# A hashed attention and feed-forward kernel on one core: the opening's weight loads, scales, filler products and first maxima rearranged

## The chip, the core and the metric

The kernel runs on one core of a Trainium2 chip. The core has five engines that run their own instruction streams in order: TensorE (PE) multiplies matrices, VectorE (DVE) and ScalarE (ACT) work elementwise, GpSimd (POOL) works elementwise too, and SyncE (SP) issues transfers. ScalarE can issue transfers as well (ACTq in the profile). The metric is the device time of one execution in microseconds; lower is better.

## What is computed

The input x has 16 batches of 512 tokens with 128 features. Each batch goes through an attention with 16 heads of 8 features and then through a feed-forward network (FFN) with a hidden width of 512:

```python
x = x + layernorm(attn(layernorm(x)))
x = x + layernorm(ffn(layernorm(x)))

def attn(x):                       # per batch and head
    q = x @ Wq.T + bq;  v = x @ Wv.T + bv
    bucket = sum over n of (q . hyperplane_n + offset_n >= 0) * 2**n
    coeff  = 62 + (bucket_i == bucket_j)
    a = softmax(q @ q.T / sqrt(128) * coeff)
    return a @ v

def ffn(x):                        # tlin(x, w, s) = (x @ w.T) * s, w ternary, s per output
    h = silu(tlin(x, w1, s1)) * tlin(x, w2, s2)
    h = gelu(tlin(h, h1, sh1));  h = gelu(tlin(h, h2, sh2))
    return tlin(h, w3, s3)
```

All is in float32, except that q is split into three bfloat16 parts for the scores.

## The kernel before

**Order.** The kernel isn't a loop nest. Processes written as generators (`prep`, `gathers`, `scores`, `coeffs`, `logits`, `maxima`, `softmax`, `attend`, `residual`, `ffn`, `weights`, `inputs`) are run by a small planner, class `Order` (L47 to L184), when the program is built. Each step names its engine, a cost in microseconds and a rank; at every moment the planner takes, on each engine that is free, the ready step of lowest rank (on ScalarE: of lowest ready time plus rank, with 4.0 added for a change of activation table), and emits its instructions. So the order of instructions on each engine, SP's transfers included, is fixed by the planner's costs. On the chip each engine follows that order and waits where its data are not there. Transfers cost the planner SP's issue time, a queue at 160 KB per microsecond and 2.6 us of latency.

**One batch.** `prep(b)` (L575) normalizes x, turns it over on TensorE, projects it to q (`qp`, L603), writes q with its bias as `qs` (L625) and as three bfloat16 parts (L708, L718, L723), each of which goes to DRAM in two layouts by two transfers (`keep`, L617). `buckets` (L628) makes the bucket numbers (`pp` L635, `bits` L647, `bkt` L662) and writes them to DRAM (`bkd`, L678). `prep` ends with v (`vp` L741, `vaug` L749). Batch 0 has its first transfer issued ahead of the planner.

**One head.** `gather(j)` (L768) fetches three tiles by SP: `ql` (L779), `qr` (L792) and the bucket row broadcast to all partitions, `bb` (L805). Four heads' tiles are there at once. For each of four groups of 128 rows, TensorE makes scores (`sp`, L827), VectorE the coefficients (`co`, L845) and the product of both with its row maxima (`l`, L874). The logits have 11 buffers of 128x2048. After two heads (`MH = 2`, L862 and L893) `maxima` (L899) turns the maxima over (`mt`, L903), writes them to DRAM (`md`, L908), and each head's `softmax` (L913) fetches them broadcast to all partitions (`mb`, L920). GpSimd subtracts them (`l`, L927), ScalarE takes the exponential (L932). After four heads `attend` (L937) multiplies by v on TensorE (`av`, L953), copies the result (`avs`, L967), turns it over (`op`, L974) and divides (L984, L985).

**After 16 heads** `residual(b)` (L998) normalizes the attention's output and adds x, in that order: mean and variance on VectorE (L423, L427), `ve` on ScalarE (L439), a power on GpSimd (`rs_o`, `rs_f`, L443), the rescaling on ScalarE (L466). Then `ffn(b)` (L1021) runs: the gates `w1` and `w2` (L1066), silu (L1052), their product (L1036), two layers `hp` (L1100) with gelu (L1113), and `yp` (L1132). Its steps on TensorE have the rank 4, behind scores (0), `av` (1) and `prep` (2). `ffn(0)` waits for the event `loaded`.

**Weights.** `weights` (L1166) loads five weights by SP, each with its scales broadcast to all partitions (L1185, L1186: 256 KB of scales for each of w1, w2, h1 and h2, 64 KB for w3), and GpSimd multiplies the scales into the weights (L1189). The first three are started at once, the last two wait for the event `gathered[3]` (`EARLY`, `LATER`). `inputs` (L503) takes the statistics of the later batches' x on ScalarE (L523, L533).

Of the kernel before, what the change touches and what calls it, by code (L numbers as in the profile page):

```python
# [46 lines left out]
class Order:  # L47
# [62 lines left out]
    def _step(self, p, value):  # L110
        while True:
            self.current = p
            try:
                want = p.gen.send(value)
            except StopIteration:
                self.live -= 1
                return
            value = None
            if want[0] == "get":
                pool = want[1]  # L120
                if not pool.free:
                    pool.waiters.append(p)
                    return
                value, deps = pool.free.pop(0)
                self._merge(p, deps)
            elif want[0] == "wait":
                if want[1].deps is None:
                    want[1].waiters.append(p)
                    return
                self._merge(p, want[1].deps)  # L130
            else:
                eng = want[1]
                when = max(
                    [self.now] + [
                        t + (self.LAT if e != eng else 0.0 if e in ("PE", "SP") else self.OWN)
                        for e, t in p.deps.items()
                    ]
                )
                self._at(when, self._offer, p, want, when)
                return  # L140
# [47 lines left out]
def tile_lsh_attention_ffn(  # L188
# [35 lines left out]
    ROOT = float(np.float32(E**-0.5))  # L224
    GROUPS = (1, 2, 6, B)
    LATE = 20
    EARLY, LATER = 2, 3
    SCALE = 1.0 / math.sqrt(E)
    AHEAD = 1
    MH = 2  # L230
# [41 lines left out]
    nc.gpsimd.memset(eps3, EPS / E**3)  # L272

    junk = const.tile([P, E], BF16, name="junk")
    warm = const.tile([P, 1], F32, name="warm")
    nc.scalar.activation(warm, eps, AF.Exp)

# [56 lines left out]
    def act(cost, rank, emit, table=None):  # L334
        return ("op", "ACT", cost, emit, rank, table)
# [239 lines left out]
    def prep(b):  # L575
# [46 lines left out]
            yield dma(256, 1, emit, cost=0.7)  # L622
            od.set(kept[i])

        yield act(0.65, -2, lambda: nc.scalar.activation(qs, qp, AF.Identity, bias=bq_sb))  # L625
        read = Event()

        def buckets():  # L628
            yield wait(read)
# [73 lines left out]

        wrote, columned = Event(), Event()
        od.spawn(buckets())
        od.set(read)
        yield act(
            0.65, -2, lambda: nc.scalar.activation(qparts[0], qp, AF.Identity, bias=bq_sb)  # L708
        )
        od.spawn(keep(0))  # L710
        yield dve(
            0.63,
            1,
# [54 lines left out]
    def gather(j, tag):  # L768
        b, h = divmod(j, H)
        yield wait(prepared[b])  # L770
        ql = p1.tile([KS, S], BF16, tag=f"ql{tag}", name=f"ql_{j}")
        qr = p1.tile([KS, S], BF16, tag=f"qr{tag}", name=f"qr_{j}")
        bb = p1.tile([P, BR * BP], BF16, tag=f"bb{tag}", name=f"bb_{j}")
        rows[j] = (ql, qr, bb, tag)

        yield dma(
            74,
            1 + j * 1e-3,
            lambda: nc.sync.dma_start(  # L779
                out=ql,  # L780
                in_=qds[b][1][h]
                .rearrange("i d s -> (i d) s")
                .unsqueeze(1)
                .to_broadcast([NP * DH, NP, S]),
            ),
            held=False,
            cost=0.75,
        )
        yield dma(
            74,  # L790
            1 + j * 1e-3,
            lambda: nc.sync.dma_start(  # L792
                out=qr,
                in_=qds[b][0][h]
                .rearrange("d j s -> (d j) s")
                .unsqueeze(0)
                .to_broadcast([NP, NP * DH, S]),
            ),
            held=False,
            cost=0.72,  # L800
        )
# [57 lines left out]
    def logits():  # L859
        for j in range(B * H):  # L860
            kl = yield get(logit_bufs)
            if j % MH == 0:  # L862
                km, pair = (yield get(mx_bufs)), []
                mx = mxpads[int(km[2:])]
            l = p1.tile([P, NT, S], F32, tag=kl, name=f"l_{j}")
            base = j % MH * NT
            for t in range(NT):
                i = j * NT + t
                yield wait(scored[i])
                yield wait(weighed[i])  # L870
# [13 lines left out]

                yield dve(0.61, 5, emit)
                od.put(score_banks, ks)
                od.put(co_bufs, kc)
                if t < NT - 1:
                    od.loose()
            od.put(row_bufs, rows.pop(j)[3])  # L890
            ls[j] = (l, kl)
            pair.append((j, l))
            if len(pair) == MH:  # L893
                od.spawn(maxima(pair, mx, km))
            if j % GH == GH - 1:
                od.spawn(attend(j // GH))
            od.loose()
# [123 lines left out]
    def ffn(b, x1, k1, xnt, kx):  # L1021
        if b:
            yield wait(stages[b - 1][AHEAD])
        yield wait(loaded)
        kh = yield get(h_bufs)
        h = p1.tile([P, NC, S], F32, tag=kh, name=f"h_{b}_0")
        there = events(NC)
# [14 lines left out]
        def silus(c0, gates, half, held):  # L1042
            for _ in gates:
                held.append((yield get(a_bufs)))
            tiles = [
                p1.tile([P, S], F32, tag=ka, name=f"a_{b}_{c0 + i}")
                for i, ka in enumerate(held)
            ]

            def emit():  # L1050
                for a, (_, gp) in zip(tiles, gates):
                    nc.scalar.activation(a, gp, AF.Silu)  # L1052

            yield act(1.2, 0, emit, "silu")
            for kb, _ in gates:
                od.put(ffn_banks, kb)
            held[:] = zip(tiles, list(held))
            od.set(half)
# [25 lines left out]
        for layer in (1, 2):  # L1084
# [5 lines left out]
            for c0 in range(0, NC, 2):  # L1090
# [16 lines left out]
                        )  # L1107
                    got.append((c, kb, hp))

                def gelus(got=got, h=h, there=there):  # L1110
# [54 lines left out]

    def weights():  # L1166

        kl = yield get(logit_bufs)
        scales = p1.tile([P, NT, S], F32, tag=kl, name="scales")
        scale3 = const.tile([P, E], F32, name="scale3")  # L1170
        folded = []
        for i, (src, scale, nk, n, name) in enumerate((
            (w1_t, w1_s, 1, HID, "w1"),
            (w2_t, w2_s, 1, HID, "w2"),
            (h1_t, h1_s, NC, HID, "h1"),
            (h2_t, h2_s, NC, HID, "h2"),
            (w3_t, w3_s, NC, E, "w3"),
        )):
            w_sb[name] = w = const.tile([P, nk, n], F32, name=name)
            sc = scales[:, i, 0:n] if i < NT else scale3  # L1180
            folded.append(Event())

            def fetch(w=w, sc=sc, src=src, scale=scale, nk=nk):
                for i in range(nk):
                    nc.sync.dma_start(out=w[:, i, :], in_=src[i * P : (i + 1) * P, :])  # L1185
                nc.sync.dma_start(out=sc, in_=scale.partition_broadcast(P))  # L1186

            def fold(w=w, sc=sc, nk=nk, n=n):
                nc.gpsimd.tensor_tensor(  # L1189
                    w, w, sc.unsqueeze(1).to_broadcast([P, nk, n]), op=ALU.mult  # L1190
                )

            def piece(fetch=fetch, fold=fold, nk=nk, n=n, done=folded[-1], i=i):
                if i > EARLY:
                    yield wait(gathered[LATER])
                yield dma(nk * n / 2 + n / 2, 3, fetch, cost=0.42 * (nk + 1))
                yield pool(nk * n / 450, 2, fold)
                od.set(done)

            od.spawn(piece())  # L1200
        for e in folded:
            yield wait(e)
        od.put(logit_bufs, kl)
        od.set(loaded)

    with tc.manual_schedule():
        for piece in (prep(0), gathers(), scores(), coeffs(), logits(), weights(), inputs()):
            od.spawn(piece)
        od.run()

# [51 lines left out]
```

## Time and profile before

| | us |
|---|---|
| median of 3 runs | 1388.59 |
| their range | 1387.49 to 1397.21 |
| the profiled execution, its own time | 1398.15 |
| its span, first to last instruction | 1396.3 |
| busy: TensorE, VectorE, GpSimd, ScalarE | 1287.3, 1235.2, 1227.3, 1110.4 |

The page gives busy time and its share of the span. Its part with 40 slices shows how this share changes in time, in tenths, and a row `PEclk` with the TensorE clock that was granted in each slice. Other views are asked for by a window in microseconds from the span's start: busy time by stretch, instructions in order of time (an entry in square brackets says how long the engine was idle before the instruction, and what ended that), and who waited for whom. Rows of SPq and ACTq are issues of transfers; their duration is that of the issue, not of the transfer.

### The profile page before, as it was taken

How to read it: one execution, taken by the hardware profiler on the slowest of the kernel's cores; microseconds unless marked ns; L12 is line 12 of the kernel's file. 1: busy time of each engine (PE TensorE's matmuls, PEld its weight loads, DVE VectorE, ACT ScalarE, POOL GpSimd, SP SyncE). 2: the span in 40 equal slices, each digit the busy share in tenths (PEclk: the TensorE clock that was granted, in tenths of full speed). 3: DMA queues.
4: the chain of work that ended last, by engine and by line, in shares of the span. 5: the costliest groups of instructions: out<-in, count | busy, mean ns of one | idle time of the engine just before them, and what ended most of it. 6: DMA issues, size and time to landing. Idle time of an engine off the chain costs nothing.

```text
span 1396.3 us, 20309 instructions
## 1 busy us (share of the span) xinstructions
PE 1287.3 (92%) x5520; PEld 521.9 (37%) x5520; DVE 1235.2 (88%) x3985; ACT 1110.4 (80%) x1608; POOL 1227.3 (88%) x322
## 2 busy tenths in 40 slices
PE   4677699899899999999999999999999999999997
PEld 1111133434344343433444334434343344433353
DVE  5978899899899999999999999999999999999220
ACT  3566789889879888988989888888888897878752
POOL 2699799989999998999999999998999899999700
PEclk9666699899999999999999999999999999999999
DMA  5655355455445445444445544454544544444100
GB/s 172 188 132 157 103 149 149 120 144 140 122 112 151 119 131 144 123 142 120 148 122 133 148 122 140 128 136 127 142 126 132 136 135 134 127 112 116 46 8 8
DMA packets 158418, 176.09 MB, mean 126 GB/s; under 512 B 32480, under 2 KB 115680, under 8 KB 158304
## 3 DMA queue, kind: packets, MB, share of 16 engines
q1 hardware_dynamic: 157872, 174.59, 45.6%
q8 instruction: 44, 0.72, 0.2%
q14 instruction: 70, 0.57, 0.2%
q10 hardware_dynamic: 432, 0.20, 0.0%
HBM read 155.59 MB, written 19.14 MB: 125 GB/s over the span
## 4 chain that ended last, share of the span: by engine, by line
PE 63%; DVE 21%; issue 6%; DMA 4%; POOL 3%; ACT 2%; SPq 0%; POOLq 0%; DVEq 0%
PE hp L1100 24%; PE av L953 16%; PE sp L827 12%; DVE l L874 10%; DVE co L845 7%; PE w L1066 3%; PE yp L1132 3%; POOL l L927 2%; DMA mb<-md 2%; PE op L974 1%; PE pp L635 1%; PE qp L603 1%; DMA ql<-qd 1%; PE vp L741 1%; ACT l L932 1%
## 5 line engine op out<-in xcount | busy, mean ns | idle before, releaser
L927 POOL TENSOR_TENSOR l<-l,mb 128x2048 f32<-128x2048 f32 x256 | 1156.3, 4552 | 36.4 <-DMA mb<-md 32.0
L874 DVE CUSTOM_DVE_ANT_0 l<-co,sp 128x512 f32<-128x512 bf16 x1024 | 666.2, 686 | 29.2 <-PE av L953 22.3
L932 ACT ACTIVATE l<-l 128x2048 f32<-128x2048 f32 x256 | 486.5, 1907 | 41.2 <-POOL l L927 40.0
L1100 PE MATMUL hp<-h,h 128*128 128x512 f32 x1024 | 495.5, 596 | 0.2 <-ACT h L1113 0.2
L845 DVE TENSOR_SCALAR co<-bb,bj 128x516 bf16<-128x516 bf16 x1024 | 454.9, 477 | 3.9 <-DMA bb<-bkd 3.8
L827 PE MATMUL sp<-qr,ql 72*128 72x512 bf16 x1024 | 378.3, 404 | 80.6 <-DVE mxpad L874 68.3
L953 PE MATMUL av<-l,vaug 128*32 128x512 f32 x2048 | 280.7, 636 | 0.4 <-DVE y L1156 0.2
L1100 PEld LDWEIGHTS hp<-h,h 128*128 128x128 f32 x1024 | 190.5, 190 | 176.0 <-issue 152.9
L827 PEld LDWEIGHTS <-ql 72*128 72x128 bf16 x1024 | 96.7, 99 | 410.6 <-issue 383.4
L1066 PE MATMUL w<-xnt_f,w 128*128 128x512 f32 x256 | 133.0, 616 | 3.2 <-ACT y L390 2.0
L932 ACT ACT_TABLE_LOAD x86 | 110.3, 1283 | 1.5
L967 ACT COPY avs<-av 128x512 f32<-128x512 f32 x64 | 37.3, 582 | 90.1 <-PE av L953 90.1
L1113 ACT ACTIVATE h<-hp 128x512 f32<-128x512 f32 x128 | 71.0, 595 | 33.9 <-PE hp L1100 33.3
L953 PEld LDWEIGHTS av<-l,vaug 128*32 128x32 f32 x2048 | 47.8, 112 | 123.0 <-issue 89.9
L874 DVE DVE_READ_ACCUMULATOR2_ANT mxpad<- 128x1 f32 x1024 | 91.6, 89 | 0.0
L1113 ACT ACT_TABLE_LOAD x58 | 74.4, 1283 | 0.8
L1132 PEld LDWEIGHTS yp<-w,h 128*128 128x128 f32 x512 | 67.0, 196 | 12.7 <-issue 8.1
L1036 DVE TENSOR_TENSOR h<-w,a 128x512 f32<-128x512 f32 x64 | 43.9, 687 | 27.8 <-PE w L1066 22.0
L1132 PE MATMUL yp<-w,h 128*128 128x128 f32 x512 | 67.9, 280 | 0.0
L1066 PEld LDWEIGHTS w<-xnt_f,w 128*128 128x128 f32 x256 | 47.6, 196 | 50.9 <-issue 21.5
L443 POOL TENSOR_TENSOR rs_y<-ve_y,mhalf 128x4 f32<-128x4 f32 x16 | 16.2, 1010 | 51.8 <-issue 34.7
L448 DVE TENSOR_SCALAR nm_y<-su_y,rs_y 128x1 f32<-128x1 f32 x64 | 9.2, 210 | 38.5 <-POOL rs_y L443 38.5
(91 smaller groups left out, 868.8 us busy)
## 6 DMA issues: line engine op xcount, KB each, us to landing
mb<-md SPq DMA_DIRECT2D x256, 256.0 KB
bb<-bkd SPq DMA_DIRECT2D x256, 130.5 KB
ql<-qd SPq DMA_DIRECT2D x256, 72.0 KB
qr<-qd SPq DMA_DIRECT2D x256, 72.0 KB
qd<-q SPq DMA_DIRECT2D x96, 128.0 KB
xta<-in_L_attn_x_dram SPq DMA_DIRECT2D x16, 256.0 KB
xtr<-in_L_attn_x_dram SPq DMA_DIRECT2D x16, 256.0 KB
out_dram<-y SPq DMA_DIRECT2D x16, 256.0 KB
```

The source lines that it names most:

```text
L827: nc.tensor.matmul(sp, lhsT=ql[:, ts(t, P)], rhs=qr, start=True, stop=True)
L845: nc.vector.tensor_scalar(co, bb.rearrange("p (r c) -> p r c", c=BP)[:, :, 0:BC], bjs[b][:, c : c + 1], float(NBKT - 2), op0=ALU.is_equal, ...
L874: nc.vector.tensor_tensor_reduce(out=l, in0=co[:, 0:S], in1=sp, scale=1.0, scalar=-3.0e38, op0=ALU.mult, op1=ALU.max, accum_out=mx[:, t : ...
L927: lambda: nc.gpsimd.tensor_tensor(l, l, mb.unsqueeze(1).to_broadcast([P, NT, S]), op=ALU.subtract),
L932: yield act(1.82, 0, lambda: nc.scalar.activation(l, l, AF.Exp, scale=SCALE), "exp")
L953: nc.tensor.matmul(av[k * Q : (k + 1) * Q, :], lhsT=va[:, t, c : c + Q], rhs=ls[gg * GH + k][0][:, t, :], start=(t == 0), stop=(t == NT - 1),)
L967: yield act(0.5, -2, lambda: nc.scalar.copy(avs, av))
L1036: lambda: nc.vector.tensor_tensor(h[:, c, :], g2, a, op=ALU.mult),
L1066: lambda: nc.tensor.matmul(gp, lhsT=w_sb[which][:, 0, ts(c, P)], rhs=xnt, start=True, stop=True),
L1100: lambda i=i: nc.tensor.matmul(hp, lhsT=w[:, i, ts(c, P)], rhs=hin[:, i, :], start=(i == 0), stop=(i == NC - 1),),
L1113: nc.scalar.activation(h[:, c, :], hp, AF.Gelu)
L1132: nc.tensor.matmul(yp[:, ts(t, E)], lhsT=h[:, i, ts(t, P)], rhs=w_sb["w3"][:, i, :], start=(i == 0), stop=(i == NC - 1),)
```

## The change

Seven edits, all about the first part of the run, except for the scales:

1. A process `activity` puts products of a zero tile into a bank of PSUM on TensorE, at rank 99, whenever the planner finds nothing else ready, from the start until `ffn(0)` begins.
2. The scales of w1, h1 and h2 are no longer multiplied into the weights: they are fetched as 128x4 tiles and given to silu and gelu as the activation's scale operand. w2 and w3 are still folded on GpSimd.
3. All weights (w2, w3, w1, h1, h2, in that order, one after another) and the two broadcast scales are issued by ScalarE, as ScalarE steps with the rank 20. h2 waits, in the planner, for `gathered[0]`.
4. The first four heads take their maxima one by one (`SINGLES = 4`).
5. In `prep(0)` VectorE writes `qs`, by an addition, instead of ScalarE.
6. The first head's `qr` is issued by ScalarE.
7. A planner request `rest` delays a process without an engine; the folds of w2 and w3 are asked for 6 us after their transfers.

```diff
@@ Order._step
+            elif want[0] == "rest":
+                self._at(self.now + want[1], self._step, p, None)
+                return
@@ constants
-    EARLY, LATER = 2, 3
+    COLD = 10.0
+    SINGLES = 4
@@ before the planner's work
+    still = const.tile([P, P], BF16, name="still")
+    nc.vector.memset(still, 0.0)
+    started = []
@@ prep
-        yield act(0.65, -2, lambda: nc.scalar.activation(qs, qp, AF.Identity, bias=bq_sb))
         read = Event()
+        def copied():
+            yield dve(0.66, 1,
+                lambda: nc.vector.tensor_scalar(qs, qp, bq_sb, None, op0=ALU.add))
+            od.set(read)
...
         od.spawn(buckets())
-        od.set(read)
+        if b:
+            yield act(0.65, -2, lambda: nc.scalar.activation(qs, qp, AF.Identity, bias=bq_sb))
+            od.set(read)
+        else:
+            od.spawn(copied())
         yield act(0.65, -2, lambda: nc.scalar.activation(qparts[0], qp, AF.Identity, bias=bq_sb))
         od.spawn(keep(0))
+        yield wait(read)
@@ gather, the transfer of qr
+        queue = nc.sync if j else nc.scalar
-            lambda: nc.sync.dma_start(out=qr, ...
+            lambda: queue.dma_start(out=qr, ...
-            cost=0.72,
+            cost=0.72 if j else 0.05,
@@ logits
-            if j % MH == 0:
+            if j < SINGLES or j % MH == 0:
                 km, pair = (yield get(mx_bufs)), []
-            base = j % MH * NT
+            base = len(pair) * NT
...
-            if len(pair) == MH:
+            if j < SINGLES or len(pair) == MH:
                 od.spawn(maxima(pair, mx, km))
@@ ffn
         yield wait(loaded)
+        started.append(b)
...
-                    nc.scalar.activation(a, gp, AF.Silu)
+                    nc.scalar.activation(a, gp, AF.Silu, scale=w_sb["w1s"][:, c : c + 1])
...
-                            nc.scalar.activation(h[:, c, :], hp, AF.Gelu)
+                            nc.scalar.activation(h[:, c, :], hp, AF.Gelu, scale=sc[:, c : c + 1])
@@ weights, rewritten
+        for layer, (src, scale, nk, n, name) in enumerate((
+            (w2_t, w2_s, 1, HID, "w2"), (w3_t, w3_s, NC, E, "w3"), (w1_t, w1_s, 1, HID, "w1"),
+            (h1_t, h1_s, NC, HID, "h1"), (h2_t, h2_s, NC, HID, "h2"))):
+            w_sb[name] = w = const.tile([P, nk, n], F32, name=name)
+            if layer == 4:
+                yield wait(gathered[0])
+            for i in range(nk):
+                yield act(0.42, LATE,
+                    lambda: nc.scalar.dma_start(out=w[:, i, :], in_=src[i * P : (i + 1) * P, :]))
+            if name in ("w2", "w3"):
...
+                yield act(0.42, LATE,
+                    lambda: nc.scalar.dma_start(out=sc, in_=scale.partition_broadcast(P)))
+                yield ("rest", 6.0)
+                yield pool(nk * n / 420, 2, lambda: nc.gpsimd.tensor_tensor(
+                        w, w, sc.unsqueeze(1).to_broadcast([P, nk, n]), op=ALU.mult))
...
+            else:
+                w_sb[name + "s"] = sc = const.tile([P, NC], F32, name=name + "s")
+                yield dma(2, 2, lambda: nc.sync.dma_start(
+                        out=sc, in_=scale.rearrange("(c p) -> p c", p=P),
+                        allow_slow_non_contiguous=True), cost=0.6)
         od.set(loaded)
@@ new process
+    def activity():
+        kb = yield get(ffn_banks)
+        bk = bank(kb, "activity")
+        def emit(start=False, stop=False):
+            nc.tensor.matmul(bk, lhsT=still,
+                rhs=still.unsqueeze(1).to_broadcast([P, NT, P]), start=start, stop=stop)
+        yield pe(0.45, 99, lambda: emit(start=True))
+        while not started:
+            yield pe(0.45 if od.now < COLD else 0.25, 99, emit)
+        yield pe(0.25, 99, lambda: emit(stop=True))
+        od.put(ffn_banks, kb)
```

More of the change, by code (lines that the diff above doesn't have):

```diff
@@ L623, in keep @@
             od.set(kept[i])
-        yield act(0.65, -2, lambda: nc.scalar.activation(qs, qp, AF.Identity, bias=bq_sb))
         read = Event()
+        def copied():
+            yield dve(
+                0.66,
+                1,
+                lambda: nc.vector.tensor_scalar(qs, qp, bq_sb, None, op0=ALU.add),
+            )
+            od.set(read)
         def buckets():
@@ L791, in gather @@
             1 + j * 1e-3,
-            lambda: nc.sync.dma_start(
+            lambda: queue.dma_start(
                 out=qr,
@@ L1050, in emit @@
             def emit():
-                for a, (_, gp) in zip(tiles, gates):
-                    nc.scalar.activation(a, gp, AF.Silu)
+                for i, (a, (_, gp)) in enumerate(zip(tiles, gates)):
+                    c = c0 + i
+                    nc.scalar.activation(a, gp, AF.Silu, scale=w_sb["w1s"][:, c : c + 1])
             yield act(1.2, 0, emit, "silu")
@@ L1108, in ffn, with gelus @@
                     got.append((c, kb, hp))
-                def gelus(got=got, h=h, there=there):
+                def gelus(got=got, h=h, there=there, sc=w_sb[f"h{layer}s"]):
                     def emit():
                         for c, _, hp in got:
-                            nc.scalar.activation(h[:, c, :], hp, AF.Gelu)
+                            nc.scalar.activation(
+                                h[:, c, :], hp, AF.Gelu, scale=sc[:, c : c + 1]
+                            )
                     yield act(1.2, 0, emit, "gelu")
@@ L1166, in weights @@
     def weights():
[L1168 to L1172, printed above, removed]
+        for layer, (src, scale, nk, n, name) in enumerate((
+            (w2_t, w2_s, 1, HID, "w2"),
+            (w3_t, w3_s, NC, E, "w3"),
             (w1_t, w1_s, 1, HID, "w1"),
-            (w2_t, w2_s, 1, HID, "w2"),
             (h1_t, h1_s, NC, HID, "h1"),
@@ L1176, in weights @@
             (h2_t, h2_s, NC, HID, "h2"),
-            (w3_t, w3_s, NC, E, "w3"),
         )):
             w_sb[name] = w = const.tile([P, nk, n], F32, name=name)
[L1180 to L1186, printed above, removed]
@@ L1188, in fold @@
-            def fold(w=w, sc=sc, nk=nk, n=n):
-                nc.gpsimd.tensor_tensor(
-                    w, w, sc.unsqueeze(1).to_broadcast([P, nk, n]), op=ALU.mult
-                )
[L1193 to L1203, printed above, removed]
-        od.set(loaded)
+            if layer == 4:
+                yield wait(gathered[0])
+            for i in range(nk):
+                yield act(
+                    0.42,
+                    LATE,
+                    lambda: nc.scalar.dma_start(out=w[:, i, :], in_=src[i * P : (i + 1) * P, :]),
+                )
+            if name in ("w2", "w3"):
+                if name == "w2":
+                    kl = yield get(logit_bufs)
+                    sc = p1.tile([P, NT, S], F32, tag=kl, name="scale2")[:, 0, :]
+                else:
+                    sc = const.tile([P, E], F32, name="scale3")
+                yield act(
+                    0.42,
+                    LATE,
+                    lambda: nc.scalar.dma_start(out=sc, in_=scale.partition_broadcast(P)),
+                )
+                yield ("rest", 6.0)
+                yield pool(
+                    nk * n / 420,
+                    2,
+                    lambda: nc.gpsimd.tensor_tensor(
+                        w, w, sc.unsqueeze(1).to_broadcast([P, nk, n]), op=ALU.mult
+                    ),
+                )
+                if name == "w2":
+                    od.put(logit_bufs, kl)
+            else:
+                w_sb[name + "s"] = sc = const.tile([P, NC], F32, name=name + "s")
+                yield dma(
+                    2,
+                    2,
+                    lambda: nc.sync.dma_start(
+                        out=sc,
+                        in_=scale.rearrange("(c p) -> p c", p=P),
+                        allow_slow_non_contiguous=True,
+                    ),
+                    cost=0.6,
+                )
@@ new lines, in weights @@
+        od.set(loaded)
+    def activity():
+        kb = yield get(ffn_banks)
+        bk = bank(kb, "activity")
+        def emit(start=False, stop=False):
+            nc.tensor.matmul(
+                bk,
+                lhsT=still,
+                rhs=still.unsqueeze(1).to_broadcast([P, NT, P]),
+                start=start,
+                stop=stop,
+            )
+        yield pe(0.45, 99, lambda: emit(start=True))
[3 more added lines that the diff above has]
+        od.put(ffn_banks, kb)
@@ L1206, in tile_lsh_attention_ffn @@
     with tc.manual_schedule():
-        for piece in (prep(0), gathers(), scores(), coeffs(), logits(), weights(), inputs()):
+        for piece in (prep(0), gathers(), scores(), coeffs(), logits(), weights(), inputs(), activity()):
             od.spawn(piece)
```

## The prediction

> **What bounds the kernel now.** I read the page first, then busy time by stretch, then the instruction order of GpSimd and SyncE up to 60 us, the waits, and ScalarE around 160 us.
>
> The page: four engines are nearly full for most of the run. The exceptions are the first slices, and TensorE's clock is at six tenths in four of them.
>
> ```profile
> PE   4677699899899999999999999999999999999997
> ...
> DVE  5978899899899999999999999999999999999220
> ...
> POOL 2699799989999998999999999998999899999700
> PEclk9666699899999999999999999999999999999999
> ```
>
> By stretch (columns: PE, PEld, DVE, ACT, POOL, clock, DMA share, GB/s): GpSimd starts late, then is full to 140 us; afterwards everybody is.
>
> ```profile
> 0.00:35.00 35.00, 15.72 (x37) 5.87 (x37) 18.47 (x68) 12.40 (x40) 9.89 (x14) 1.00 0.56 172
> 35.00:70.00 35.00, 22.92 (x49) 6.75 (x49) 34.60 (x104) 17.62 (x51) 23.36 (x6) 0.64 0.67 187
> 70.00:105.00 35.00, 25.31 (x103) 6.25 (x103) 27.22 (x87) 22.02 (x44) 35.00 (x10) 0.70 0.51 132
> 105.00:140.00 35.00, 27.44 (x107) 6.28 (x106) 29.28 (x88) 21.55 (x38) 35.00 (x8) 0.69 0.59 161
> 140.00:175.00 35.00, 23.88 (x77) 6.63 (x77) 30.47 (x109) 24.82 (x53) 27.87 (x9) 0.61 0.39 101
> ```
>
> Per batch GpSimd needs 16 subtractions of 4.552 us and three powers of 1.01, 75.9 us. VectorE needs about 75 (16 heads of 4.0, from 24.57 to 29.4 less the first coefficients, and about 11 of the rest). A batch takes (1317.6 - 52.4)/16 = 79.1 us between the first subtraction's start and the last one's end. So GpSimd's chain of subtractions sets the pace, VectorE close behind, and the question is when it begins and where it stands still. In order of time:
>
> ```profile
> 39.86 4.51 POOL L1189 TENSOR_TENSOR h<-h,scales 128x2048 f32<-128x2048 f32 x1 [20.93 <-DMA w<-in_L_ffn_w_w_dram]
> 44.33 1.27 POOL L1189 TENSOR_TENSOR w<-w,scale 128x512 f32<-128x512 f32 x1
> 52.37 9.01 POOL L927 TENSOR_TENSOR l<-l,mb 128x2048 f32<-128x2048 f32 x2 [6.78 <-DMA mb<-md]
> ...
> 34.85 0.56 SPq L908 DMA_DIRECT2D md<-mt  x1
> ...
> 37.74 2.31 SPq L1185 DMA_DIRECT2D w<-in_L_ffn_w_w_dram  x4
> ...
> 46.34 0.56 SPq L908 DMA_DIRECT2D md<-mt  x1
> ...
> 48.10 1.09 SPq L920 DMA_DIRECT2D mb<-md  x2
> ```
>
> The first pair's maxima leave at 34.85, but SP's order puts the w3 weights, gathers and prep(1)'s writes ahead of fetching them back at 48.10; the first subtraction starts at 52.37. The second place is 155 to 162 us: GpSimd idles 7.03 us at `rs_f`, because ScalarE stands at `avs`, ahead of `ve_f` in its order, for `av` at the half clock (8 products 1.87 us apart there, 16 in 1.85 us elsewhere).
>
> ```profile
> 161.38 0.58 ACT L967 COPY avs<-av 128x512 f32<-128x512 f32 x1 [6.55 <-PE av L953]
> 161.86 0.30 ACT L439 ACTIVATE ve_f<-mv_f,eps 128x4 f32<-128x4 f32 x1
> ...
> 162.23 1.01 POOL L443 TENSOR_TENSOR rs_f<-ve_f,mhalf 128x4 f32<-128x4 f32 x1 [7.03 <-ACT ve_f L439]
> ```
>
> **The change part by part.** *The road to the first coefficients* (24.57 us). With `qs` on VectorE, ScalarE starts `q0` when its squares end (12.31) and not at 13.27: -1.0. `q2` no longer waits behind `bits` (15.96, its input ready at 15.35): -0.6. SP loses the first `qr` issue (0.77) ahead of `bb`: -0.8. A warm clock shortens `qp` (2.09 us for a product; 0.86 later on), but ScalarE's squares hold `q0` there anyway: 0 on this road, cover named. Moved to ScalarE are 16 issues of weights and broadcast scales at 0.40 to 0.47 (rows of L248 to L252), 7 us, and the `qr`. What falls ahead of `q0` and `q1` is between 0 and the four issues of w3, 1.8 us; the planner starts them only when ScalarE is free, so I take 0.5. Sum -1.9: coefficients from 22.7.
>
> *The weights off SP and GpSimd.* SP sheds about 9.4 us of issues (L1185, L1186) and takes three columns of scales (0.6 each, as L258). GpSimd sheds folds of 4.50, 4.51 and 1.27, all before 46 us. The h2 fold would now be in the way, so it is worth something only together with the next part. The weights' bytes stay (the broadcast scales fall by 0.75 MB), and h1 and h2 move into the window of the first maxima.
>
> *The maxima one by one.* Head 0's logits take 4.85 us from the first coefficient (24.57 to 29.4), so 27.6, `mt` to 27.8. From an `md` issue to a subtraction the one row there is 46.34 to 52.37, 6.0 us; with h1 and h2 beside it I take 7.2 (bounds 5.5, a shorter queue, and 12, 1 MB at the stretch's 187 GB/s in front of it). First subtraction: 35.0. The four singles run to 53.2. Heads 4 and 5 are a pair again: VectorE ends head 5 at 27.8 + 5 x 4.15 (4.03 and the `mt`) + 2.35 (prep(1)'s L647, L714, L723, L699) = 50.9, so their subtraction starts at 58.1: GpSimd stalls 4.9 us there. From then on it is fed (head 7 ends at 59.9, plus 7.2, 67.1; GpSimd is free at 67.2). Counted back by four subtractions, 58.1 is a start of 39.9 against 52.37: **-12.5**. The bounds of the 7.2 hold for the pair too and move the sum by -1.7 and +4.8.
>
> A rule against this part: the Trainium skill ("DMA: Bandwidth & Descriptors", section "Issuing engines are not separate DMA queues") says that issuing from several engines saves only the sequencer's time, since all share the same 16 DMA engines. By that alone the move is worth SP's 9.4 us and the transfers no less; the SP rows above say that here it is the order of issue that held `mb` back.
>
> *The filler.* It isn't in the trace. The nearest row is a warm score product of the same 512 columns: 0.38 alone, 0.60 for two, so 0.22 from one to the next; the planner counts 0.25. Some 1.9 us of each head's 4.55 are real TensorE work at warm clock (four scores, a quarter of `av` and `op`), and prep comes on top, so until about 150 us there is room for some 85 us, 340 products. At 0.22 TensorE runs ahead of the plan and the filler costs nothing; cover: idle time. With a held clock the four `av` steps after 152.5 take 4 x (0.93 + 0.22) in place of 8.8, `avs` stands 4.2 earlier, `rs_f` 4.0: **-4.0** (bounds 0, if the clock stays half, and -7.0, the whole stall). What is late next there is `mv_f`, done at 157.1. The waits of VectorE for `av` (12.9 us to 170) fall too, but behind GpSimd.
>
> The Trainium skill ("TensorE: Matmul & The Clock Gate", section "Terms") prices a throttle at throttled time times the lost share. The stretches from 35 to 175 us have 95 us at half clock, so by the page 48 us; the rows say 4, since TensorE isn't the bound there.
>
> *Scales in activations.* An operand per partition costs ScalarE: 680 ns (L625, with one) against 582 (L967, without), 0.098 us, on 192 silus and gelus: 18.8 us, 1.2 per batch, where ScalarE has 8 to 10 idle. ScalarE makes 2% of the chain; 2% of it is 0.4, which I take; bounds 0 and 18.8. Two more `mt` on VectorE, 0.4, beside GpSimd's work: 0.
>
> Sum: 12.5 + 4.0 - 0.4 = 16.1. VectorE allows it: 1.9 earlier, and its idle time of 17.4 us before 170 (7.7, 5.2 and 4.5 in the waits) goes, 19.3. The rest of the run is shifted. The profiled execution would go from 1398.15 to 1382.0; it lies 9.6 above the median of the timed runs, so the median goes from 1388.6 to **1372.5**.
>
> **The rivals.**
> 1. *Eaten on the way.* Beyond 170 us VectorE, TensorE and GpSimd are all above 95% busy, and GpSimd waits 32.0 us on `mb` in all. VectorE enters with a lead of 4 to 5 heads and not the full buffers of before (3.10 us wait at 98 for a free one), and every engine's order is drawn anew. 0.6 us more per batch is 10: 1382. Against it: the same loads as before, and the order's costs hardly change.
> 2. *The filler blocks TensorE (slower).* Products queued for an idle time can't be overtaken. If each costs more than planned, the lateness adds up until `ffn(0)`. Break-even: 16.1/340 = 0.047 above 0.25, about 0.30. At 0.32 (0.22 and an uncovered weight load, 0.099) it is 24 us late: 1396; at a clock that stays half (0.42) 58 late: 1430. Against it: weight loads of scores lie beside the products.
> 3. *More than that.* The whole `rs_f` stall goes and the pair's stall is halved: 12.5 + 2.5 + 7.0 = 22; VectorE's allowance is 19.3, and less waiting at the half clock after 170 (0.80 from 245 to 280) may add 4: 1366.
> 4. *It doesn't do what it says*: clock stays low without blocking, or `mb` lands at the 12 us bound: 1372.5 + 4.0 + 4.8, 1381.
>
> **How the numbers follow.** A measurement of this kernel can tell about 1% (13.9 us) from no change; below 1374.7 is faster, above 1402.5 slower. Forecast (own range 1367 to 1378) 0.45, of it 0.36 faster; rival 3 0.18, faster; rivals 1 and 4 together 0.24, of it 0.04 faster; rival 2 0.13, of it 0.10 slower. Faster 0.58, same 0.32, slower 0.10. The range leaves out rival 2's slower part and the outer half of rival 3: 1362 to 1390.
>
> **What would show it.** First subtraction near 35 us and a gap of some 5 us ahead of the fifth; first coefficients near 22.7; clock near full from 40 to 170; GpSimd's wait at the first `rs_f` 3 us or less; silus and gelus near 690 ns; last subtraction some 16 us earlier. The prediction is wrong if fillers stand ahead of scores that VectorE waits for, if `mb` still lands after 45 us, or if the batches after 170 us take longer than 79.1 us.

## The result and the profile after

| kernel | median, us | ratio to the kernel before (95%) | profiled span, us | mean clock |
|---|---|---|---|---|
| before, run beside the result | 1391.70 | | 1396.3 | 0.947 |
| after | 1372.83 | 0.9862 (0.9838 to 0.9887) | 1371.3 | 0.991 |

The median fell by 18.9 us. The profiled execution of the changed kernel took 1373.08 us, that of the kernel before 1398.15, a difference of 25.1; the kernel before happened to be profiled in one of its longer executions. The prediction had 16.1 for both.

The page, its busy tenths and the granted clock: the weak first slices of TensorE and the stretch at six tenths of the clock are gone, and so is GpSimd's dip to seven tenths in its fifth slice. Near the end GpSimd has less left in its last three slices than before (4, 0 and 0 tenths in place of 7, 0 and 0), while TensorE is full to the last one, as it was before.

```profile
PE   9999999999889999999999999999999999999996
...
DVE  5999999999889999999999999999999999998210
...
POOL 1599999999999999999999999999999999999400
PEclk9999999999899999999999999999999999999998
```

The stretches up to 175 us (columns: PE, PEld, DVE, ACT, POOL, clock, DMA share, GB/s). Before, the clock was 0.61 to 0.70 from 35 us on; it is 1.00 now, and TensorE is busy nearly without a break, much of that with filler. The 1.00 of the first stretch is not the same in the two traces: the kernel before has no record of the clock ahead of 41.4 us, and its first scores, at 24 to 25 us, take 0.59 to 0.63 us each; in the changed kernel the records begin at 5.5 us, and those scores take 0.38.

```profile
0.00:35.00 35.00, 32.37 (x135) 13.68 (x135) 18.10 (x66) 9.55 (x31) 5.43 (x13) 1.00 0.52 148
35.00:70.00 35.00, 33.74 (x151) 14.31 (x154) 33.90 (x103) 19.46 (x52) 20.22 (x5) 1.00 0.70 189
70.00:105.00 35.00, 33.94 (x181) 12.71 (x172) 33.00 (x105) 22.77 (x45) 35.00 (x9) 1.00 0.55 147
...
140.00:175.00 35.00, 34.55 (x177) 12.67 (x175) 34.33 (x117) 26.39 (x53) 35.00 (x10) 1.00 0.50 145
```

GpSimd in order of time. The first subtraction starts at 40.46 (52.37 before), but the first four stand apart: there are waits for `mb` ahead of the second, third and fourth. The stall at `rs_f` (7.03 before) is gone.

```profile
40.46 4.52 POOL L947 TENSOR_TENSOR l<-l,mb 128x2048 f32<-128x2048 f32 x1 [21.18 <-DVE mxpad L894]
47.58 4.53 POOL L947 TENSOR_TENSOR l<-l,mb 128x2048 f32<-128x2048 f32 x1 [2.61 <-DMA mb<-md]
53.62 4.54 POOL L947 TENSOR_TENSOR l<-l,mb 128x2048 f32<-128x2048 f32 x1 [1.50 <-DMA mb<-md]
63.18 4.52 POOL L947 TENSOR_TENSOR l<-l,mb 128x2048 f32<-128x2048 f32 x1 [5.02 <-DMA mb<-md]
67.89 22.61 POOL L947 TENSOR_TENSOR l<-l,mb 128x2048 f32<-128x2048 f32 x5 [0.18 <-DVE co L865]
...
143.82 13.58 POOL L947 TENSOR_TENSOR l<-l,mb 128x2048 f32<-128x2048 f32 x3
157.36 1.00 POOL L450 TENSOR_TENSOR rs_f<-ve_f,mhalf 128x4 f32<-128x4 f32 x1
```

Head by head, these are the starts of subtractions in the two traces:

| head (from 0) | before | after | gain |
|---|---|---|---|
| 0 | 52.37 | 40.46 | 11.9 |
| 4 | 70.3 | 67.9 | 2.4 |
| 16 | 127.1 | 124.8 | 2.3 |
| 24 | 172.2 | 162.8 | 9.4 |
| 80 | 450.2 | 436.1 | 14.1 |
| 255 | 1313.1 | 1277.0 | 36.1 |
| end of span | 1396.3 | 1371.3 | 25.0 |

So most of the opening's 11.9 us are gone by the fifth head, another 7 come at `rs_f`, and 22 more between head 80 and head 255, where the code of the two kernels differs in nothing but the scale operands. Of the 36 at the last head, 11 are given back in the tail: behind the end of the last subtraction the kernel before needs 78.7 us, the changed one 89.8. The tail is TensorE's. GpSimd's last rows show it idle for 22 us and then 35, while TensorE makes feed-forward products (15 and 35 in the kernel before):

```profile
1328.58 1.01 POOL L450 TENSOR_TENSOR rs_y<-ve_y,mhalf 128x4 f32<-128x4 f32 x1 [22.27 <-ACT ve_y L446]
1364.26 1.01 POOL L450 TENSOR_TENSOR rs_y<-ve_y,mhalf 128x4 f32<-128x4 f32 x1 [34.67 <-issue]
```

TensorE's rows for that time run into each other:

```profile
1324.60 4.65 PE L1088 MATMUL w<-xnt_f,w 128*128 128x512 f32 x10
1329.08 27.63 PE L1122 MATMUL hp<-h,h 128*128 128x512 f32 x64
1356.55 3.66 PE L1156 MATMUL yp<-w,h 128*128 128x128 f32 x28
```

The later batches differ in order. Compared instruction by instruction, the programs show two recurring orders. In the first, *order A* (the kernel before), GpSimd mostly has two or three subtractions between `rs_o` and `rs_f` of a batch; in about half of the batches it stands still there, as here:

```profile
1180.99 1.00 POOL L443 TENSOR_TENSOR rs_o<-ve_o,mhalf 128x4 f32<-128x4 f32 x1
1182.03 9.06 POOL L927 TENSOR_TENSOR l<-l,mb 128x2048 f32<-128x2048 f32 x2
1194.04 1.01 POOL L443 TENSOR_TENSOR rs_f<-ve_f,mhalf 128x4 f32<-128x4 f32 x1 [2.95 <-ACT ve_f L439]
```

In *order B* (the changed kernel, from its fifth batch on), `rs_y` of the batch before comes directly behind `rs_o`, and four or five subtractions follow:

```profile
1153.34 1.01 POOL L450 TENSOR_TENSOR rs_o<-ve_o,mhalf 128x4 f32<-128x4 f32 x1
1154.32 1.01 POOL L450 TENSOR_TENSOR rs_y<-ve_y,mhalf 128x4 f32<-128x4 f32 x1
1155.29 18.05 POOL L947 TENSOR_TENSOR l<-l,mb 128x2048 f32<-128x2048 f32 x4
1173.76 1.01 POOL L450 TENSOR_TENSOR rs_f<-ve_f,mhalf 128x4 f32<-128x4 f32 x1 [0.42 <-ACT ve_f L446]
```

The experiments had to tell apart: the prediction's account (the opening's gain and `rs_f`, carried along unchanged), the filler and its clock, and an *order theory*: that the changed opening tips the planner into another order for the rest of the run, and that this order is worth much of the gain.

### The profile page after: what moved, and what is told of

It reads as the page before. It is cut to its first block, busy times and chain, and to the rows that moved or that the text cites. A ratio compares the mean times of both kernels' runs of the same rounds, so it can differ in the third digit from the quotient of the medians.

```text
span 1371.3 us, 21177 instructions
## 1 busy us (share of the span) xinstructions
PE 1317.3 (96%) x5922; PEld 550.9 (40%) x5922; DVE 1236.0 (90%) x3989; ACT 1127.8 (82%) x1607; POOL 1217.1 (89%) x319
## 4 chain that ended last, share of the span: by engine, by line
PE 50%; DVE 24%; POOL 9%; issue 8%; DMA 6%; ACT 2%; SPq 1%; POOLq 0%; DVEq 0%; ACTq 0%
PE hp L1122 18%; PE av L973 12%; DVE l L894 11%; PE sp L847 9%; DVE co L865 8%; POOL l L947 8%; PE w L1088 4%; PE yp L1156 3%; DMA mb<-md 3%; DMA bb<-bkd 1%; DMA qd<-q 1%; PE op L994 1%; PE vp L760 1%; POOL rs_x L561 1%; DMA qr<-qd 1%
## 5 line engine op out<-in xcount | busy, mean ns | idle before, releaser
L894 DVE CUSTOM_DVE_ANT_0 l<-co,sp 128x512 f32<-128x512 bf16 x1024 | 665.7, 681 | 13.8 <-PE av L973 6.9
L847 PE MATMUL sp<-qr,ql 72*128 72x512 bf16 x1024 | 358.0, 382 | 26.7 <-DVE mxpad L894 22.5
L973 PE MATMUL av<-l,vaug 128*32 128x512 f32 x2048 | 263.6, 603 | 0.0
L1251 PE MATMUL activity<-still 128*128 128x512 bf16 x402 | 106.6, 385 | 1.0 <-DVE still L280 1.0
L894 DVE DVE_READ_ACCUMULATOR2_ANT mxpad<- 128x1 f32 x1024 | 85.7, 84 | 0.0
L450 POOL TENSOR_TENSOR rs_y<-ve_y,mhalf 128x4 f32<-128x4 f32 x16 | 16.1, 1006 | 67.1 <-issue 34.7
L1251 PEld LDWEIGHTS <-still 128*128 128x128 bf16 x402 | 39.1, 99 | 56.5 <-issue 19.0
```

What stands on the lines that cost most here:

```text
L847: nc.tensor.matmul(sp, lhsT=ql[:, ts(t, P)], rhs=qr, start=True, stop=True)
L894: nc.vector.tensor_tensor_reduce(out=l, in0=co[:, 0:S], in1=sp, scale=1.0, scalar=-3.0e38, op0=ALU.mult, op1=ALU.max, accum_out=mx[:, t : ...
L973: nc.tensor.matmul(av[k * Q : (k + 1) * Q, :], lhsT=va[:, t, c : c + Q], rhs=ls[gg * GH + k][0][:, t, :], start=(t == 0), stop=(t == NT - 1),)
L1251: nc.tensor.matmul(bk, lhsT=still, rhs=still.unsqueeze(1).to_broadcast([P, NT, P]), start=start, stop=stop,)
```

## The experiments

All medians are in us. e1 to e4 ran beside one another and share a median of 1394.05 for the kernel before; so do e5 to e8 (1393.44), and e9 and e10 (1392.14). The changed kernel itself, 1372.83, was timed apart; e4 (1373.53) and e8 (1372.2) equal it within their intervals and stand in for it where a difference of a few microseconds is taken beside e1, e2 or e6.

| label | kernel | order of later batches | median | ratio to before (95%) |
|---|---|---|---|---|
| e1_order_no_filler | after, filler planned and not emitted | B, as after | 1380.24 | 0.9905 (0.9887 to 0.9924) |
| e2_pairs | after, maxima in pairs | A | 1384.21 | 0.9934 (0.9914 to 0.9955) |
| e3_before_filler | before, filler added | A, as before | 1389.9 | 0.9978 (0.9964 to 0.9992) |
| e4_no_scale_operand | after, no scale operand (the scales of w1, h1 and h2 are left out) | B, as after | 1373.53 | 0.9855 (0.9833 to 0.9876) |
| e5_before_other_order | before, h2 one gather earlier | a mixture | 1390.51 | 0.9983 (0.9969 to 0.9998) |
| e6_qs_on_scalar | after, `qs` back on ScalarE | near A | 1388.25 | 0.9964 (0.995 to 0.9979) |
| e7_weights_later | after, w1 and h1 wait too | B | 1374.39 | 0.987 (0.9847 to 0.9894) |
| e8_sixteen_single | after, 16 single heads | B | 1372.2 | 0.9847 (0.9825 to 0.9868) |
| e9_before_both | e5 with filler | as e5 | 1385.23 | 0.9946 (0.9928 to 0.9965) |
| e10_qs_scalar_eight_single | e6 with 8 single heads | B | 1372.5 | 0.986 (0.9836 to 0.9883) |

### e1: the changed kernel without its filler

The planner still plans all 402 filler steps, so every engine's order is that of the changed kernel; 401 of them put nothing on TensorE.

```diff
-        yield pe(0.45, 99, lambda: emit(start=True))
+        yield pe(0.45, 99, lambda: emit(start=True, stop=True))
-            yield pe(0.45 if od.now < COLD else 0.25, 99, emit)
-        yield pe(0.25, 99, lambda: emit(stop=True))
+            yield pe(0.45 if od.now < COLD else 0.25, 99, lambda: None)
+        yield pe(0.25, 99, lambda: None)
```

> The changed kernel with the order of every engine as it is, but only one filler product emitted, so TensorE idles where the other 401 stood. Theory 1 (the clock): the filler's warm clock gives back the 7 us stall at the first rs_f and the first batches' waits for av, so without it about 10 us come back: 1383 us, and the clock is near 0.95 again. Theory 2 (the new order of the later batches gives the time, the filler little): 1375 us. Theory 3 (the fillers cost something): below 1372 us.

Measured: 1380.24, 7.4 above the changed kernel and 6.7 above e4 of the same call, so the filler is worth about 7 us; and the changed kernel without it is still 13.8 below the kernel before of the same call (1394.05). The stretch around `rs_f` has the low clock of before again:

```profile
140.00:175.00 35.00, 23.49 (x83) 5.04 (x82) 32.79 (x118) 25.05 (x52) 35.00 (x10) 0.66 0.44 126
```

and still GpSimd doesn't stall there, since the changed order has three subtractions ahead of `rs_f`:

```profile
144.58 13.54 POOL L947 TENSOR_TENSOR l<-l,mb 128x2048 f32<-128x2048 f32 x3
158.07 1.02 POOL L450 TENSOR_TENSOR rs_f<-ve_f,mhalf 128x4 f32<-128x4 f32 x1
```

The filler's 7 us therefore don't come by way of that stall, which was the prediction's reason for them. They don't show in the opening's subtractions either: e1's start within 1 us of the changed kernel's at the heads 0, 4, 16 and 24, and 9.3 us later at head 80.

### e2: maxima in pairs again

```diff
-    SINGLES = 4
+    SINGLES = 0
```

> The changed kernel with the first four heads' maxima in pairs again (SINGLES = 0). Prediction's step (one by one is worth most of 12.5 us at the start): first subtraction about 4 us later and 5 to 8 us lost, 1379 us. Rival (the trace shows the fifth head's subtraction only 2.4 us earlier than before, since the order of SyncE holds the fourth head's maxima back): within 3 us of the changed kernel, 1371 to 1376 us.

Measured: 1384.21, so 11.4 of the gain go (10.7 against e4). In the opening, little does: the first subtraction starts at 44.5, that of head 4 at 70.3 (67.9 with singles), and the first batch's output is turned over for `ffn(0)` earlier than in the changed kernel (`tp_f` at 161.2 against 163.3). The later batches have order A: by the names in the traces, the last 5137 of TensorE's 5520 products and the last 3493 of VectorE's instructions stand in the sequence of the kernel before; and heads 80 to 255 take 860.0 us, as before (862.9), in place of 840.9. So the single maxima can't be priced by this run alone: they change the order of everything behind them.

### e3: the kernel before with filler

In the planner, ahead of each TensorE step of the kernel before, the idle time that it has just passed is filled with products of zeros into a spare bank; the order stays that of the kernel before.

```diff
+        if eng == "PE" and self.fill is not None:
+            self.fill(self.now, self.now - self.until[eng])
...
+    def fill(now, idle):
+        if started:
+            return
+        for _ in range(int(idle / (0.45 if now < 10.0 else 0.25))):
+            nc.tensor.matmul(spare, lhsT=still, ...
```

> The kernel before with the order of every engine as it was, and 386 filler products put into the idle time that the planner saw on TensorE before the first feed-forward stage. Theory 1 (the clock): the rs_f stall of 7 us goes, 8 to 12 us faster than before, 1381 us. Theory 2 (order): 2 to 4 us faster, 1388 us. Rival 2 of the prediction (fillers block TensorE): slower than before, above 1395 us.

Measured: 1389.9 against 1394.05 (0.9978, interval 0.9964 to 0.9992): 4 us, the size that the prediction gave to the filler. The stall at `rs_f` is gone here too, now without any change of order:

```profile
148.91 9.06 POOL L933 TENSOR_TENSOR l<-l,mb 128x2048 f32<-128x2048 f32 x2
157.94 1.00 POOL L449 TENSOR_TENSOR rs_f<-ve_f,mhalf 128x4 f32<-128x4 f32 x1
```

The clock in that stretch is 1.00:

```profile
140.00:175.00 35.00, 33.31 (x170) 11.90 (x168) 34.43 (x121) 29.09 (x56) 35.00 (x10) 1.00 0.45 131
```

So the clock and the changed program's order each remove that stall by themselves. And with the clock at 1.00 in the opening, order A still gives 1390: the filler is not what makes the other 15 us. Nor is the order all of it: e2, in order A and with filler too, lies 5.7 us below e3. What e2 has beside that are the other edits (weights on ScalarE, scales in the activations, `qs` and the first `qr`); no run takes these apart.

### e4: the scale operand

```diff
-                    nc.scalar.activation(a, gp, AF.Silu, scale=w_sb["w1s"][:, c : c + 1])
+                    nc.scalar.activation(a, gp, AF.Silu)
...
-                                h[:, c, :], hp, AF.Gelu, scale=sc[:, c : c + 1]
+                                h[:, c, :], hp, AF.Gelu
```

> The changed kernel, same order, silu and gelu without the scale operand (the scales of w1, h1 and h2 are left out of the result). Prediction's step: ScalarE falls by 192 x 0.098 = 18.8 us of busy time and the end moves by 0 to 1 us, 1372 us. Rival (ScalarE's added time stands on the path of the later batches): 5 to 15 us faster, 1358 to 1368 us.

Measured: 1373.53, within 1 us of the changed kernel. In the groups by line (busy us, mean ns, then idle time before them), a gelu takes 684 ns with the operand:

```profile
L1135 ACT ACTIVATE h<-hp,h1s 128x512 f32<-128x512 f32 x64 | 41.2, 684 | 12.6 <-PE hp L1122 12.1
```

and 595 without:

```profile
L1135 ACT ACTIVATE h<-hp 128x512 f32<-128x512 f32 x128 | 70.7, 595 | 32.6 <-PE hp L1122 31.9
```

That is 89 ns on 192 instructions, 17 us of ScalarE, and none of it reaches the end.

### e5 and e9: another order for the kernel before

To see whether the order alone pays, the kernel before was given another one by starting h2 a gather earlier; that gives GpSimd's later batches the sequence of order B in part, with a transition of its own early on. e9 adds the filler of e3.

```diff
-    EARLY, LATER = 2, 3
+    EARLY, LATER = 2, 2
```

> The kernel before with one number changed, LATER = 2: the loads of h2 and w3 wait in the planner for the third head's gather and not for the fourth's. It moves a few transfers by some microseconds early on, and from the fourth batch on the planner settles into the order of the changed kernel, in which GpSimd takes rs_y right behind rs_o. Order theory: about 11 us of the changed kernel's gain is that order, so 1383 us here. Rival (the later batches gain from what the edits do on the chip: activations with scales, weights, a warm start): within 3 us of before, 1391 to 1397 us.

> The kernel before with two additions only: LATER = 2 (the other order of the later batches) and the filler in the planner's idle time on TensorE, every engine's order as in the run with LATER = 2 alone. No single maxima, no scales in activations, weights still on SyncE. If the two effects are independent: the filler brings 8 to 11 us up to 450 us of the run on top of the order's 3 net, 1380 us. If filler and order together are the changed kernel's whole gain (the traces put 9 us of TensorE's work before 450 us and 16 after): 1374 to 1378 us. If the other edits carry a good part: above 1384 us.

Measured: 1390.51 against 1393.44 (0.9983, interval 0.9969 to 0.9998), 2.9 faster where the order theory had 11; and with filler 1385.23, 6.9 faster than before, about the sum of e3's 4 and e5's 3. Most of the gain between the heads 80 and 255 does appear in e5 (847.3 us against 862.9), but its tail is longer, as the changed kernel's is: 88.5 us behind the last subtraction against 78.7. Early on it gains nothing (head 16 starts 3.9 us later than before, head 80 less than 1 us earlier). The order theory in its simple form, "whatever has order B gains 11", failed here. e9 falls where its expectation said that the other edits carry a good part (above 1384). Its order is the mixture and not order B, though, so e9 can't tell what the other edits give from what the mixture lacks.

### e6 and e10: `qs` back on ScalarE

```diff
-        if b:
+        if True:
```

> The changed kernel with qs of the first batch back on ScalarE; everything else, the filler and the single maxima too, stays. The planner then ends up in the order of before in the later batches. Prediction's step: 1 us on the road to the first coefficients, so 1374 us. Order theory: like the run with pairs, 1384 us.

e10 is e6 with `SINGLES = 8`, which by the program leads into order B again:

> The changed kernel with qs of the first batch on ScalarE, as in the run that fell back to 1388 us, and eight single maxima in place of four, with which the planner settles into the order of the changed kernel again. Order theory: 1371 to 1375 us. If qs on VectorE is worth something by itself: 1380 us or more.

Measured: e6 1388.25, 15 us lost (16 against e8 of the same call) by one activation of 0.67 us in the first batch, more than the order theory gave it and far from the prediction's step. e10, with the same activation in the same place, 1372.5: nothing lost. This pair is the clearest: with this edit in both, the ratios are 0.9964 and 0.986, and what differs is the number of single heads and with it the order of all later batches. Since e8 shows that more single heads gain nothing by themselves where the order is B already, the order is what is left.

### e7: the weights later

w1 and h1 wait, as h2 does, for the first gather.

```diff
-            if layer == 4:
+            if layer >= 2:
```

> The changed kernel with w1, h1 and h2 all waiting in the planner for the first gather, so that h1's 1 MB isn't under way while the first head's tiles are fetched. The later order is that of the changed kernel. The first coefficients start at 22 to 23 us and not at 25.5. If the opening's microseconds carry through: 1369 us; if SyncE's order around the fourth head takes them back: 1373 us.

Measured: 1374.39, no change that can be told from the changed kernel. Its opening did become earlier: the first coefficients start at

```profile
24.30 1.65 DVE L865 TENSOR_SCALAR co<-bb,bj 128x516 bf16<-128x516 bf16 x4 [1.46 <-DMA bb<-bkd]
```

in e7, and at

```profile
25.45 1.65 DVE L865 TENSOR_SCALAR co<-bb,bj 128x516 bf16<-128x516 bf16 x4 [2.83 <-DMA bb<-bkd]
```

in the changed kernel; the first subtraction stands at 38.3 against 40.5. Two microseconds at the first head are worth nothing at the end.

### e8: sixteen single heads

```diff
-    SINGLES = 4
+    SINGLES = 16
```

> The changed kernel with the first 16 heads' maxima one by one (SINGLES = 16); the later order is that of the changed kernel. Order theory: 1371 to 1374 us. If single maxima as such are what gives 11 us: 1365 us or less, since there are four times as many.

Measured: 1372.2 (0.9847, interval 0.9825 to 0.9868), the same as the changed kernel within the intervals. The first subtraction is at 40.6, the order is B. No version tried is faster than the changed kernel by an amount that can be told.

## Why the prediction came out right, and where its steps did not

The total was right; the reasons were right in part. Step by step:

**What bounds the kernel: failed.** "GpSimd's chain of subtractions sets the pace" described the opening. It doesn't set the end: 36 us at the last subtraction became 25 at the end, because the feed-forward products behind it had to be done anyway. TensorE's fixed work sets the end. Three differences from the kernel before can be read in each trace: how much earlier TensorE starts the transposes `tp_f` that turn the first batch over, its last step there ahead of `ffn(0)`; how much less half clock it has between that and its last product (half of that time counts, as products then take about twice as long: eight `av` products 1.94 us in place of 1.07); and how much less it idles there, filler counted as idle. Before has `tp_f` at 170.2, 48.7 us of half clock and 38.9 of idle time:

```profile
170.18 1.06 PE L482 MATMUL tp_f<-ident,xn_f 128*128 128x128 f32 x4
```

| kernel | `tp_f` at | earlier | half clock behind it | counts | idle | counts | sum | span shorter by |
|---|---|---|---|---|---|---|---|---|
| e2 | 161.2 | 9.0 | 37.5 | 5.6 | 40.2 | -1.3 | 13.3 | 11.0 |
| e3 | 165.2 | 5.0 | 30.7 | 9.0 | 42.0 | -3.0 | 11.0 | 8.5 |
| e6 | 160.1 | 10.1 | 41.0 | 3.9 | 43.6 | -4.7 | 9.3 | 6.9 |
| e1 | 168.6 | 1.6 | 23.4 | 12.6 | 38.1 | 0.8 | 15.0 | 17.5 |
| e10 | 161.8 | 8.4 | 17.1 | 15.8 | 38.5 | 0.4 | 24.6 | 26.4 |
| after | 163.3 | 6.9 | 17.1 | 15.8 | 38.9 | 0.0 | 22.7 | 25.1 |
| e9 | 164.1 | 6.1 | 27.3 | 10.7 | 38.8 | 0.1 | 16.9 | 11.6 |
| e5 | 171.1 | -0.9 | 24.7 | 12.0 | 37.2 | 1.7 | 12.8 | 6.6 |

The sum is 2.3 to 2.5 us too large for the three kernels in order A or near it and 1.8 to 2.5 too small for the three in order B; for e9 and e5 it is 5 and 6 too large, which stays unexplained. So it is an account to within some 2.5 us, not a proof. For the changed kernel it says: about 7 us from the opening, about 16 from less half clock behind `tp_f`. Not all of the 16 is the order's: e3, in the order of before, has 30.7 us of half clock there in place of 48.7, and only the filler is new in it.

**Road to the first coefficients, -1.9: failed.** They came at 25.45, 0.9 later than before. `bb` was issued at 20.08, 1.15 earlier than before (21.23), but from that to its first use passed 5.4 us (3.3 before), beside `h1` from the other queue; e7, which holds `h1` back, needs 4.0 and has them at 24.30. The microsecond that `qs` on VectorE was to bring isn't there either: e6, with `qs` on ScalarE, has them at 24.78. SyncE's and ScalarE's queues in order of time:

```profile
20.08 0.41 SPq L825 DMA_DIRECT2D bb<-bkd  x1
...
19.88 0.34 ACTq L1207 DMA_DIRECT2D w<-in_L_ffn_w_w_dram  x1
20.27 0.97 ACTq L1207 DMA_DIRECT2D h<-in_L_ffn_h_w_dram  x2
```

The rule of the Trainium skill that the prediction quoted against the change ("DMA: Bandwidth & Descriptors", section "Issuing engines are not separate DMA queues") agrees with this: `h1` was issued by another engine than `bb`, and `bb` still came 1.4 us faster in e7, without `h1` beside it. e7 also shows that it had no price at the end.

**Maxima one by one, -12.5: the term of the sum that failed.** The first subtraction was 11.9 earlier (40.46; 35.0 predicted), but at the fifth head 2.4 were left. The gap of 5 us that was predicted ahead of the fifth head came one head earlier and for another reason. The fourth head's maxima were turned over at 46.95:

```profile
46.95 0.21 DVE L923 STREAM_TRANSPOSE mt<-mxpad 128x32 f32<-128x32 f32 x1
```

but SP's order sent them on only at 52.31 and put the fetch behind another two heads' gathers:

```profile
52.31 0.54 SPq L928 DMA_DIRECT2D md<-mt  x1
...
58.17 0.56 SPq L928 DMA_DIRECT2D md<-mt  x1
...
59.60 0.39 SPq L940 DMA_DIRECT2D mb<-md  x1
```

This is the fault that the prediction had read from the rows of before at 34.85 and 48.10; it took it for cured, and it had moved three heads on. The pair's length was worked out as if transfers left when their data were ready.

**Filler, -4.0: the size nearly right, the path wrong.** The clock went to 1.00, the 402 products (106.6 us of TensorE) delayed nothing that the end shows, and rival 2 did not occur. It is worth about 7 in the changed kernel's order (e1) and 4 in that of before (e3). The path was to be the stall at `rs_f`; e1 has that stall gone without filler and is some 7 slower all the same. What e1 has worse in the table is `tp_f`, 5.3 us later, and 6.3 us more half clock right behind it. The clock rule that was weighed (the Trainium skill, "TensorE: Matmul & The Clock Gate", section "Terms": throttled time times the lost share) would give, as an estimate, 48 us for the stretches up to 175; the trace's account gives 7, because TensorE had idle time there. Behind `tp_f`, where it idles for 39 us of some 1200, the table counts by the same rule (half of 31.6 us less half clock) and comes within 2.4 us of the span.

**Scales, 0.4: right.** 89 ns where 98 were taken, and the end within 1 us.

**"The rest of the run is shifted": failed, and it is where the missing gain came from.** Per head the later batches take 840.9/175 = 4.805 us in place of 862.9/175 = 4.931. Rival 1 had said that every engine's order is drawn anew, and had the sign wrong: the new order is the better one. In order A batches have a stretch in which TensorE has little but score products, one at a time, as VectorE empties a bank (around 986, 1068, 1147 and 1226 us in the kernel before). The last of these:

```profile
1225.92 0.38 PE L827 MATMUL sp<-qr,ql 72*128 72x512 bf16 x1 [0.57 <-DVE mxpad L874]
1226.53 0.38 PE L827 MATMUL sp<-qr,ql 72*128 72x512 bf16 x1 [0.23 <-DVE mxpad L874]
1227.91 0.38 PE L827 MATMUL sp<-qr,ql 72*128 72x512 bf16 x1 [1.01 <-DVE mxpad L874]
1228.22 1.07 PE L953 MATMUL av<-l,vaug 128*32 128x512 f32 x8
...
1229.76 1.94 PE L953 MATMUL av<-l,vaug 128*32 128x512 f32 x8
```

Half the clock follows, from 1229.2 to 1232.6: eight `av` products take 1.94 us in place of 1.07.

```profile
1230.00:1234.00 4.00, 4.00 (x22) 0.56 (x18) 3.93 (x12) 1.04 (x1) 4.00 (x3) 0.67 0.21 57
```

The kernel before has seven such dips of 3.4 us between 597 and 1301 us, about one per batch from 990 on; the changed one has its last, apart from the end, at 671.1. Between the starts of the heads 80 and 255 the kernels in order A or near it have 17 to 24 us of half clock and take 860 to 863 us; those in order B have 0 to 3.4 and take 839 to 841. Between 1000 and 1100 us order A has the clock at 0.98 in the kernel before

```profile
1000.00:1100.00 100.00, 97.54 (x439) 40.32 (x438) 97.07 (x306) 82.64 (x102) 95.07 (x25) 0.98 0.49 135
```

and order B has 1.00, with more VectorE and ScalarE work done in the same 100 us (after):

```profile
1000.00:1100.00 100.00, 98.81 (x437) 40.37 (x439) 99.03 (x324) 89.21 (x109) 97.31 (x28) 1.00 0.48 134
```

That the order and not an edit carries this is shown by e6 against e10, and by e2 against e8. That the dips make the difference at the end is only the account above, and they can't be all of the 22 us at head 255: half of 20 us is 10, and 11 come back in the tail. e5 and e9 also have only 0 to 3.4 us of half clock between these heads and take 847. A filler in just these stretches of the kernel before would test it; it wasn't tried, as all eight banks of PSUM are in use there.

**The sum.** 16.1 was made of 12.5 and 4.0. On the runs it is about 7 for the filler (e1), and most of the other 12 of 18.9 hang on the order: e2, in order A with the filler, loses 11. The parts don't simply add up: e3, e2 and e9 show filler 4 us in order A, all edits but the single maxima 9.8 there, and filler with the mixture 6.9; what the other edits give by themselves stays open. A gain in the opening that SP took back and a gain in the later order that wasn't foreseen happen to be of one size. That is luck, and the working did not make the total right.

## What to carry to other kernels

When a planner writes the order, a small edit changes the order of the whole program: compare the two programs' orders before pricing an edit by its own instructions, and test an edit in two different orders (e6 and e10) before believing what it costs. A gain at the head of a chain is only as large as what is left at the last engine with fixed work; follow it from head to head to the end, and look at the tail. Ask of each early transfer not only whether its data are ready but when its queue's order lets it go, the second and third time too.

## What the runs showed of the hardware

The clock falls not only in long idle times. In the rows from 1225.9 to 1228.2 us of the kernel before, TensorE had single score products of 0.38 us, 0.6 to 1.4 us apart, with no idle time above 1.01 us between them, and was granted half the clock from 1229.2 to 1232.6. e2 and e3, with the same order there, have five and four such dips behind 550 us in place of seven, so not every such stretch is followed by one.

402 products of zeros, put in only where the planner saw nothing else ready, were enough to keep the granted clock at 1.00 from 5.5 us, where its record begins, to 175 us; in e1, with the same order and one of them, it is 0.65 to 0.70 from 35 us on. The first ten, which start ahead of 5.2 us, took 0.61 to 0.63 us each; from 5.58 us on one takes 0.38.
